# The first sorting in twelve held pieces, the reflections in a list of their own, and the fourth modulation over the dense stage

## The chip, the cores and the metric

The kernel runs on one core of one Trainium2 chip. A core has a matrix engine (PE, with its weight loads PEld), a vector engine (DVE), a scalar engine (ACT) and GpSimd (POOL). SP only issues DMAs, and POOL issues some too. Each engine works off its own queue in order, and semaphores tie the queues together. The metric is the device time of one execution in microseconds (us). The kernel before takes 1922.47 us, the median of three runs (1920.68 to 1925.31).

## The reference

Four blocks follow one another on `x`, 4 batches of 512 tokens of 288 features, with a condition row `c` for each batch:

```python
# block 0: attention, then a mixture of experts (4 experts, 2 for each token)
mod = silu(c) @ w_adaln + b_adaln              # six rows: shift, scale, gate, twice
x = x + g_msa * attention(ln(x) * (1 + sc_msa) + sh_msa)
xf = ln(x) * (1 + sc_mlp) + sh_mlp
cw = softmax over the top 2 of (xf @ w_gate), 0 for the other two
x = x + g_mlp * sum_e cw[e] * (gelu(xf @ w1[e] + b1[e]) @ w2[e] + b2[e])
# block 1: attention, then a dense MLP, modulated in the same way
# block 2: rotation in a subspace
U = qr(P).Q                                    # P is 288 x 64
R = expm(A - A.T), A's upper triangle = silu(c) @ W.T + b   # 64 x 64 for each batch
x = x + ((x @ U) @ R - x @ U) @ U.T
# block 3: as block 1, with LayerNorm weights ln1_w, ln1_b, ln2_w, ln2_b
```

Block 2's `qr` and `expm` don't depend on `x`: the kernel works them off in small pieces beside the blocks before. The six rows of `mod` of each block are as free.

## The kernel before

**Attention** (`attention`, run for blocks 0, 1 and 3 with names `a0`, `a1`, `a3`). There are 16 groups, 4 batches by 4 groups of 4 heads. A pass `r` computes the row maxima of group `r`, and the exponentials and sums of groups `r - 1` and `r - 2`. A pass has 8 gaps `k`. In each, `quad` puts two score tiles for maxima (`a0m`, reduced by DVE at L986) and two for weights (`a0s`, exponentials on ACT at L998) into four PSUM banks. Then come the pass's `steps[k]` and its `pieces`: letters that stand for generators advanced by one `yield` each (`Q` queries and keys, `X` values or projection, `A` transposed activations, `R` the sorting). Each pass ends with `shift`, four transposes (`a0sh`) that also mark passes in a trace. A tail of five steps follows pass 15: it finishes the last sums, starts the next feed's first chunks and the last projections.

**The feed** is what an attention hands over to: `Experts` after the first, `Dense` after the second and third. In `others` a feed streams matrix columns, and `went` calls `tick` each time that a number of columns, its pace, has passed.

**Side work.** `tick(works)` advances the first generator of a list by one `yield`. There are two lists: `beside`, begun with `rotation()`, and `aside`, begun with `exponential()`. In attention a tick of `beside` comes at some gaps (`ticks`: 4 a pass in the first attention, 2 from pass 10 on, 2 in the second), and in its tail. `rotation()` is 64 Householder reflections, then `subspace()` (the U of the reflections by a doubling of block sizes) and four products `ue`. A reflection's dots run on DVE, its root on POOL (`nrm`, L633; on DVE among the experts, where `far` is set); then DVE finishes it, and SP spreads a row over partitions (`v<-pT`, L550), which `reflect` applies on DVE. `modulation(l)` loads its matrix in six pieces, multiplies, and lays biases and LayerNorm rows out by many small DMAs on POOL's queue (`short_rows`, `features`: eight DMAs a table).

**Sorting.** `ranked(b)` computes a batch's gate logits and ranks, in 6 pieces; `placed(h)` counts how many tokens of a half of the batches each expert has, gives every token its slot, and issues the gathers (indirect DMAs on POOL) of the first experts' weights and tokens, in 6 pieces. The first half is sorted in passes 11 to 15 of the first attention, the second among the experts.

**Order.** A scheduler lays out each engine's queue from a model of times. What the kernel fixes: matmuls issued through `mm` stay in their order; `take(engine, i)` notes an instruction, and `beside_of(engine, j)` puts `j` behind the last one noted on that engine. The row maxima are noted for DVE. An instruction with neither can be placed ahead of a row maximum that comes before it in the program.

Of the kernel before, what the change touches and what calls it, by code (L numbers as in the profile page):

```python
# [8 lines left out]
F32 = mybir.dt.float32  # L9
# [37 lines left out]
def kernel(ctx: ExitStack, tc: tile.TileContext, a: dict, out: bass.AP):  # L47
# [53 lines left out]
    def beside_of(engine, instruction):  # L101
        if engine in taken:
            ordered(instruction.ins, taken[engine])

# [105 lines left out]
    def short_rows(dst, src, name, queue, got=None):  # L210

        n = src.shape[1]
        turned = small.tile([CP, KC, n], F32, tag=f"turned{n}", name=f"{name}t", bufs=1)
        early = got is not None
        if not early:
            got = small.tile([CP, n, KC], F32, tag=f"short{n}", name=f"{name}s", bufs=1)
            beside_of(queues.get(queue), queue.dma_start(got, src))
            beside_of("DVE", nc.vector.tensor_copy(turned, got.rearrange("p n k -> p k n")))
        else:
            in_turn("ACT", nc.scalar.copy(turned, got.rearrange("p n k -> p k n")))  # L220
# [102 lines left out]
    def modulation(l):  # L323
# [14 lines left out]
        def half(i):  # L338

            pieces, whole = [], l > 0 or i > 0  # L340
            if f"lnw{l}" in a:
                lnw = wt.tile([P, MC + 1, 2], F32, tag="lnw", name=f"lnw{l}_{i}")
                lnb = wt.tile([P, MC + 1, 2], F32, tag="lnb", name=f"lnb{l}_{i}")
                short_rows(lnw, a[f"lnw{l}"], f"lnw{l}_{i}", queue)
                short_rows(lnb, a[f"lnb{l}"], f"lnb{l}_{i}", queue)
            if whole and i == 0:
                nc.sync.dma_start(gate, a[f"adag{l}"].partition_broadcast(B))
            for n in range(3):
# [5 lines left out]
                if whole:  # L354
                    yield
            if i == 0:
# [214 lines left out]

    def reflect(k, m, v, n):
# [4 lines left out]
        nc.vector.scalar_tensor_tensor(w2[0:n], w, -1.0, c, ALU.mult, ALU.mult)  # L577
        nc.vector.scalar_tensor_tensor(
# [22 lines left out]
    def reflections():  # L601
# [14 lines left out]
        for k in range(RK):  # L616
# [27 lines left out]
            if n > 1:  # L644
                v = reflector("v", k)
                yield
                yield
                if far[0]:
                    yield
                    yield  # L650
                reflect(k, pT, v, n - 1)
# [229 lines left out]
    beside, aside = [rotation()], [exponential()]  # L881
# [7 lines left out]
    def attention(l, w, mod, eps, feed, ticks, hT=None, then=None, also=()):  # L889
# [11 lines left out]
        with ExitStack() as es:  # L901
# [353 lines left out]
            for r in range(1, n):  # L1255
# [4 lines left out]
                for k in range(gaps):  # L1260
# [17 lines left out]
                    if k % 2 and (k + 3) % (gaps // some) == 0:  # L1278
                        tick()

# [3 lines left out]
            for k in range(NT + 1):  # L1284
# [10 lines left out]
                if k < NT and k % (NT // ticks) == 0:  # L1295
                    tick()
            inside[0] = False
# [26 lines left out]
    class Feed:  # L1324
# [41 lines left out]

        def went(self, columns):
            for n, pace in enumerate(self.paces):
                self.streamed[n] += 0 if self.alone else columns
                if self.streamed[n] >= pace:  # L1370
                    self.streamed[n] -= pace
                    tick((beside, aside)[n])
# [134 lines left out]
    class Dense(Feed):  # L1507


        paces = (900,)  # L1510
# [47 lines left out]
    class Experts(Feed):  # L1558
# [90 lines left out]
        def modulated(self, b):  # L1649
# [20 lines left out]
            def scaled(t):  # L1670
# [7 lines left out]
                nc.vector.scalar_tensor_tensor(  # L1678
                    o, o, rstd[:, t : t + 1], rows["sh"], ALU.mult, ALU.add
                )  # L1680
                nc.vector.tensor_copy(
# [69 lines left out]
        def placed(self, h):  # L1751
# [7 lines left out]

            sel, upto = t3("sel", [HT, E]), t3("upto", [HT + 1, E])  # L1760
            nc.vector.tensor_scalar(sel, rank, 2.0, 1.0, ALU.is_lt, ALU.mult)
            nc.vector.memset(upto[:, 0, :], 0.0)
            for t in range(HT):
                nc.vector.tensor_add(upto[:, t + 1, :], upto[:, t, :], sel[:, t, :])
# [14 lines left out]
            def slots_of(o, v, n):  # L1779
# [3 lines left out]
                nc.vector.tensor_tensor(  # L1783
# [5 lines left out]
                nc.vector.tensor_reduce(o, over, AX.X, ALU.add)  # L1789

            def before(o, v):
                prior = t3("prior", [E, E])
                nc.vector.tensor_mul(prior, earlier, v.unsqueeze(1).to_broadcast(wide4))
                nc.vector.tensor_reduce(o, prior, AX.X, ALU.add)
# [5 lines left out]
            if h == 0:  # L1800

                taken, a_ = t3("taken", [E]), t3("a", [E])
                nc.vector.tensor_scalar_add(left, count, 1.0 - SW)
                slots_of(used, left, HB * T // SW)
                before(at, used)
                nc.vector.tensor_scalar(taken, at, -1.0, float(NF0), ALU.mult, ALU.add)
                nc.vector.scalar_tensor_tensor(taken, taken, 0.0, used, ALU.max, ALU.min)
                nc.vector.scalar_tensor_tensor(left, taken, -float(SW), count, ALU.mult, ALU.add)
                slots_of(g, left, HB * T // SW)
                before(starts[:, 0:E], g)  # L1810
                nc.vector.tensor_scalar(
                    a_, at, float(NF0), float(SW), ALU.min, ALU.mult
                )
                nc.vector.tensor_scalar_mul(b, taken, float(SW))
                nc.vector.tensor_scalar(
                    d, starts[:, 0:E], float(NF0), float(SW), ALU.add, ALU.mult
                )
                nc.vector.tensor_sub(d, d, b)
                nc.vector.tensor_sub(d, d, a_)
                firsts = at  # L1820
            else:
                nc.vector.tensor_add(used, left, count)
                slots_of(at, used, 2 * HB * T // SW)
                nc.vector.tensor_sub(used, at, g)
                before(at, used)
                nc.vector.scalar_tensor_tensor(d, at, float(SW), lk, ALU.mult, ALU.add)
                nc.vector.tensor_add(
                    starts[:, E : 2 * E], at, self.starts[:, 2 * E :].to_broadcast([P, E])
                )
                a_, b, firsts = la, lb, starts  # L1830
            pos, ge = t3("pos", [HT, E]), t3("ge", [HT, E])
# [4 lines left out]
            nc.vector.tensor_tensor(ge, ahead[:, 0:HT, :], each(b), ALU.is_ge)  # L1836
            nc.vector.tensor_mul(ge, ge, each(d))
            nc.vector.tensor_add(pos, ahead[:, 0:HT, :], each(a_))
            nc.vector.tensor_add(pos, pos, ge)
            yield  # L1840
            two, of = t3("pj", [2, HT]), t3("of", [HT, E])
            for j in range(2):
                for o, i in ((two[:, j, :], pos), (self.two[h][:, j, :], cw)):
                    nc.vector.scalar_tensor_tensor(
                        of, rank, float(j), i, ALU.is_equal, ALU.mult
                    )
                    nc.vector.tensor_reduce(o, of, AX.X, ALU.add)
            nc.vector.tensor_copy(self.place[h], two)
# [3 lines left out]
            nc.vector.tensor_tensor(  # L1852
# [5 lines left out]
            nc.vector.tensor_reduce(e, past, AX.X, ALU.add)  # L1858
            if h == 1:
                nc.vector.scalar_tensor_tensor(  # L1860
                    e, past[:, :, E - 1], -float(E), e, ALU.mult, ALU.add
                )
            nc.vector.tensor_copy(self.erow[h][:, 0:ns], e)
            nc.vector.scalar_tensor_tensor(
# [7 lines left out]
            if h == 0:  # L1872

                nc.vector.scalar_tensor_tensor(
                    la, starts[:, 0:E], float(SW), left, ALU.mult, ALU.add
                )
                nc.vector.scalar_tensor_tensor(lb, g, float(SW), left, ALU.mult, ALU.subtract)
                total = self.starts[:, 2 * E :]
                nc.vector.tensor_add(total, starts[:, E - 1 : E], g[:, E - 1 : E])
                nc.vector.tensor_add(lk, starts[:, 0:E], g)  # L1880
                nc.vector.tensor_sub(lk, total.to_broadcast([P, E]), lk)
                nc.vector.tensor_scalar_mul(lk, lk, float(SW))
# [9 lines left out]
            nc.vector.tensor_tensor(  # L1892
# [623 lines left out]
```

## Time and profile before

| | us |
|---|---|
| median of three runs | 1922.47 |
| the profiled execution, device time | 1925.5 |
| its span | 1923.8 |
| PE busy in the span | 1866.2 |
| first attention: first transposes of pass 0 to those of pass 15 (46.2 to 392.4) | 346.2 |
| second attention, the same (870.4 to 1190.2) | 319.8 |
| third attention, the same (1425.1 to 1740.8) | 315.7 |
| dense stage of block 1 after its first batch (1250 to 1385.7) | 135.7 |

A windows row reads: stretch from the span's start, its length, then busy time and number of instructions of each engine, the granted clock of PE, the DMA share and GB/s. "PE idle" and waits are what the trace shows between instructions of an engine, with what ended the wait. The three attentions have the same matrix work; the first and second also carry side work.

### The profile page before, as it was taken

What the parts mean: (1) busy time and instruction counts of PE and PEld (TensorE: products, weight loads), DVE (VectorE), ACT (ScalarE), POOL (GpSimd) and SP (SyncE); (2) the same over time, 40 slices, a digit from 0 to 9 for tenths busy, and PEclk for the clock granted to TensorE, in tenths of its full rate; (3) what the DMA queues carried; (4) which work ended last, traced back from release to release, by engine and by line L of the source; (5) the groups of instructions that cost most, each with busy time, mean ns of one, the idle gap of its engine ahead of it and who ended that gap; (6) DMA issues with size and microseconds to landing.
All of it is one profiled execution on the core that took longest, in us unless ns stands there. A gap on an engine that the chain in (4) does not pass through costs nothing. (4 is left out here: it accounts for less than half of the span.)

```text
span 1923.8 us, 28245 instructions
## 1 busy us (share of the span) xinstructions
PE 1866.2 (97%) x10385; PEld 993.9 (52%) x10385; DVE 1069.5 (56%) x3158; ACT 736.2 (38%) x1353; POOL 526.5 (27%) x766
## 2 busy tenths in 40 slices
PE   7999999989999999999999999999999999999998
PEld 4434444446767777774344443555654444433565
DVE  4677777735534555657867668152265666563201
ACT  1554554443322222324455555221134555455120
POOL 3021322234334347622313023112501121222101
PEclk9999999889989999999999999999999999999999
DMA  7421122325677667631211111300001111111000
GB/s 147 103 46 34 17 58 56 87 53 166 192 213 208 176 186 219 198 101 28 50 30 30 27 28 26 73 15 5 23 1 16 39 32 24 29 28 22 19 18 23
DMA packets 86988, 136.93 MB, mean 71 GB/s; under 512 B 32291, under 2 KB 67662, under 8 KB 86850
## 3 DMA queue, kind: packets, MB, share of 16 engines
q1 hardware_dynamic: 63554, 61.46, 14.3%
q0 software_dynamic: 23184, 73.66, 13.3%
q8 instruction: 82, 1.34, 0.3%
q14 instruction: 56, 0.46, 0.1%
q10 hardware_dynamic: 112, 0.01, 0.0%
HBM read 103.25 MB, written 20.08 MB: 64 GB/s over the span
## 5 line engine op out<-in xcount | busy, mean ns | idle before, releaser
L986 DVE TENSOR_REDUCE max<-a3m 128x1 f32<-128x512 f32 x256 | 164.7, 686 | 121.6 <-PE a3s L79 114.8
L986 DVE TENSOR_REDUCE max<-a1m 128x1 f32<-128x512 f32 x256 | 164.3, 684 | 88.2 <-PE a1s L79 82.1
L986 DVE TENSOR_REDUCE max<-a0m 128x1 f32<-128x512 f32 x256 | 165.2, 684 | 85.8 <-PE a0s L79 72.5
L998 ACT ACTIVATE a0p<-a0s 128x512 f32<-128x512 f32 x256 | 140.7, 596 | 155.2 <-PE a0s L79 155.0
L998 ACT ACTIVATE a1p<-a1s 128x512 f32<-128x512 f32 x256 | 140.0, 596 | 139.1 <-PE a1s L79 139.1
L998 ACT ACTIVATE a3p<-a3s 128x512 f32<-128x512 f32 x256 | 139.7, 596 | 135.5 <-PE a3s L79 135.5
L79 PE MATMUL e0h<-e0hT,e0w 128*128 128x256 f32 (+1 forms) x918 | 171.4, 400 | 2.3 <-ACT e0hT L2073 0.7
L79 PE MATMUL e0o<-e0w,e0hm 128*128 128x288 f32 x648 | 168.3, 409 | 2.4 <-DVE ef L854 2.4
L79 PE MATMUL a0m<-a0qk,a0qk 32*128 32x512 f32 x512 | 163.8, 649 | 6.6 <-DVE max L986 5.2
L79 PE MATMUL a0s<-a0qk,a0qk 32*128 32x512 f32 x512 | 166.5, 653 | 0.0
L79 PE MATMUL a1m<-a1qk,a1qk 32*128 32x512 f32 x512 | 153.3, 640 | 3.2 <-DVE max L986 1.8
L79 PE MATMUL a1s<-a1qk,a1qk 32*128 32x512 f32 x512 | 154.5, 639 | 0.0
L79 PE MATMUL a3m<-a3qk,a3qk 32*128 32x512 f32 x512 | 151.2, 640 | 2.3 <-ACT a3qk L969 0.8
L79 PE MATMUL a3s<-a3qk,a3qk 32*128 32x512 f32 x512 | 152.5, 640 | 0.0
L79 PEld LDWEIGHTS e0h<-e0hT,e0w 128*128 128x128 f32 (+1 forms) x918 | 130.5, 193 | 37.4 <-issue 16.7
L79 PEld LDWEIGHTS e0o<-e0w,e0hm 128*128 128x128 f32 x648 | 120.0, 190 | 33.9 <-DVE ef L854 3.1
L1424 ACT ACTIVATE e0hm<-e0h,e0w 128x256 f32<-128x256 f32 x144 | 60.1, 471 | 127.3 <-PE e0h L79 108.0
L633 POOL TENSOR_TENSOR nrm<-n,phalf 64x1 f32<-64x1 f32 (+34 forms) x35 | 19.3, 550 | 289.4 <-DVE n L628 289.4
L1984 POOL DMA_INDIRECT e0w<-w1c,wrow x57 | 55.6, 976 | 117.0 <-PE e0h L79 50.9
L79 PEld LDWEIGHTS a0m<-a0qk,a0qk 32*128 32x128 f32 x512 | 48.9, 185 | 68.8 <-DVE max L986 35.0
L79 PE MATMUL f1h<-f1hT,w 128*128 128x512 f32 (+1 forms) x216 | 81.3, 616 | 0.4 <-ACT f1hT L509 0.4
L79 PE MATMUL f3h<-f3hT,w 128*128 128x512 f32 (+1 forms) x216 | 79.4, 613 | 0.4 <-ACT f3hT L509 0.4
(532 smaller groups left out, 3184.9 us busy)
## 6 DMA issues: line engine op xcount, KB each, us to landing
eo<-e0r SPq DMA_DIRECT2D x50, 144.0 KB
ada<-in_ada SPq DMA_DIRECT2D x18, 324.0 KB
wr<-in_wrot SPq DMA_DIRECT2D x16, 288.0 KB
xm<-e0m SPq DMA_DIRECT2D x6, 768.0 KB
g<-gates SPq DMA_DIRECT2D x24, 144.0 KB
w<-in_w SPq DMA_DIRECT2D x6, 432.0 KB
x<-in_x SPq DMA_DIRECT2D x16, 144.0 KB
w1c<-in_w SPq DMA_DIRECT2D x8, 288.0 KB
```

What stands on the lines that cost most here:

```text
L79: ins = nc.tensor.matmul(*args, **kwargs).ins
L633: in_turn("POOL", nc.gpsimd.tensor_tensor(nrm, n2, phalf[0:n], ALU.pow))
L986: take("DVE", nc.vector.tensor_reduce(m[:, t, i, D : D + 1], ps, AX.X, ALU.max))
L998: take("ACT", nc.scalar.activation(p, ps, AF.Exp, scale=D**-0.5))
L1424: nc.scalar.activation(self.hms[i][f], ps[r], func, bias=b1(f)),
L1984: gather = nc.gpsimd.indirect_dma_start(dst, None, table, bass.IndirectOffsetOnAxis(row, 0))
```

## The change

**A list for the reflections.** `beside` begins empty and `rotation()` is in a new list, `turning`. In attention a tick of `turning` comes at gaps 1 to 6 of each pass for which `feed.turns(r)` holds and at which no `R` stands: passes 3 to 13 of the first attention and none in its tail, passes 5 to 15 of the second and two at each of the four steps of its tail. A reflection has one more `yield` before `reflect` (among the experts one of two extra ones goes in exchange, so five stay) and, inside an attention, one in the middle of `reflect` and one after it: six instead of three there, four instead of three in the dense stage. `went` ticks `turning` and `aside`; the dense stage's paces are 780 and 1900 columns, from one of 900.

**The fourth modulation** (`modulation(3)`) goes to `aside`, from `beside`, so that it runs beside the rotation over the dense stage. Its LayerNorm tables are loaded by POOL, copied on DVE some yields later, and spread one table a `yield`.

**The sorting.** `placed` has 12 pieces in place of 6, with these places for `R`:

```diff
-            if r == 13:
+            if r == 12:
                 loaded, steps = self.modulated(1)
                 loaded()
-                spaced([lambda k=k: (steps[k](), steps[k + 1]()) for k in range(0, 2 * NT, 2)])
+                spaced([lambda: None] * (NT - 1) + steps[0:NT])
+                self.scaled = steps[NT:]
+                pieces = {0: "XXX", 2: "XXQ", 3: "QQQ", 4: "QQQ", 6: "QQ"}
+            if r == 13:
+                spaced(self.scaled)
             more = {
                 11: {0: "R", 3: "R", 6: "R", 7: "R"},
-                12: {0: "R", 4: "R"},
-                13: {6: "R", 7: "R"},
-                14: {0: "R", 2: "R", 4: "R", 6: "R", 7: "R"},
-                15: {0: "R", 2: "R", 3: "R", 4: "R", 7: "R"},
+                12: {0: "R", 2: "R"},
+                13: {4: "R", 5: "R", 6: "R", 7: "R"},
+                14: {k: "R" for k in range(2 * NT)},
+                15: {k: "R" for k in range(6)},
             }.get(r, {})
```

**Held.** The DVE instructions of `choose`, `placed` and half of `modulated` go through `behind`, which puts each behind the last one noted on DVE. In the first sorting the running counts `upto` move from DVE to POOL, and a small copy of `modulated` (96 elements a partition) moves from DVE to ACT for the first two batches.

```diff
+    class Behind:
+        def __init__(self, engine, name):
+            self.engine, self.name = engine, name
+        def __getattr__(self, operation):
+            def one(*args, **kwargs):
+                ins = getattr(self.engine, operation)(*args, **kwargs)
+                beside_of(self.name, ins)
+                return ins
+            return one
+    behind = Behind(nc.vector, "DVE")
...
-    beside, aside = [rotation()], [exponential()]
+    turning, beside, aside = [rotation()], [], [exponential()]
...
+                    if 0 < k < gaps - 1 and feed.turns(r) and "R" not in pieces.get(k, ""):
+                        tick(turning)
...
+                for _ in range(2 if k < NT and feed.turns(n) else 0):
+                    tick(turning)
...
-                    tick((beside, aside)[n])
+                    tick((turning, aside)[n])
...
     class Dense(Feed):
-        paces = (900,)
+        paces = (780, 1900)
+        def turns(self, r):
+            return r > NG
...
+            other = nc.gpsimd if h == 0 else behind
-            nc.vector.tensor_scalar(sel, rank, 2.0, 1.0, ALU.is_lt, ALU.mult)
-            nc.vector.memset(upto[:, 0, :], 0.0)
+            behind.tensor_scalar(sel, rank, 2.0, 1.0, ALU.is_lt, ALU.mult)
+            other.memset(upto[:, 0, :], 0.0)
             for t in range(HT):
-                nc.vector.tensor_add(upto[:, t + 1, :], upto[:, t, :], sel[:, t, :])
+                other.tensor_add(upto[:, t + 1, :], upto[:, t, :], sel[:, t, :])
...
+        def turns(self, r):
+            return 2 < r < B * NG - 2
...
     mod, work = modulation(3)
-    beside.append(work)
+    aside.append(work)
...
     feed.finish()
+    while turning:
+        tick(turning)
     while beside:
         tick()
```

The old method `turns` of `Experts` is called `upright`. Among the experts the list of fine steps takes the twelve pieces of the second `placed` in the places of its six.

## The prediction

> **What bounds the kernel now.** First the busy shares and the clock of the page.
>
> ```profile
> PE 1866.2 (97%) x10385; PEld 993.9 (52%) x10385; DVE 1069.5 (56%) x3158; ACT 736.2 (38%) x1353; POOL 526.5 (27%) x766
> PEclk9999999889989999999999999999999999999999
> ```
>
> PE is busy for 97% of the span, so a gain must come from PE's idle time, from its slow stretches, or from matmuls that stretch while another engine is late. The clock dips in three places. The view of waits, PE alone, has the idle time:
>
> ```profile
> PE a0m L79 <- DVE max L986: 5.2, 9, 1.9
> PE e0xt L79 <- DVE a0r L1320: 4.6, 1, 4.6
> PE psr L786 <- DMA wr<-in_wrot: 3.4, 1, 3.4
> ```
>
> Then windows: the first attention's passes 1 to 14 and the third's, their last passes, and stretches of 3.41 us around the dips (stretch, length, busy us of PE, PEld, DVE, ACT, POOL; the clock stands third from the end).
>
> ```profile
> 46.20:359.40 313.20, 309.06 (x1919) 131.42 (x1917) 233.17 (x608) 157.44 (x280) 59.42 (x101) 1.00 0.23 52
> 1425.10:1721.00 295.90, 292.99 (x1817) 123.04 (x1815) 179.80 (x322) 153.14 (x272) 49.55 (x85) 1.00 0.14 27
> 359.40:392.40 33.00, 29.48 (x150) 13.38 (x149) 23.86 (x81) 10.37 (x19) 12.14 (x15) 0.79 0.44 116
> 1721.00:1740.80 19.80, 19.26 (x115) 6.51 (x113) 15.54 (x36) 9.78 (x18) 7.72 (x12) 1.00 0.13 18
> 369.17:372.58 3.41, 1.22 (x6) 0.40 (x6) 3.34 (x12) 0.45 (x1) 3.11 (x6) 1.00 0.93 287
> 372.58:386.24 13.66, 13.66 (x52) 6.56 (x56) 8.12 (x17) 2.92 (x6) 6.16 (x7) 0.50 0.56 165
> 406.72:410.13 3.41, 0.00 (x0) 0.00 (x0) 0.16 (x1) 1.30 (x4) 0.22 (x1) 1.00 0.42 40
> 410.13:420.37 10.24, 9.11 (x38) 2.46 (x38) 0.40 (x2) 1.46 (x3) 0.79 (x1) 0.50 0.14 15
> 734.39:737.80 3.41, 1.76 (x7) 1.44 (x8) 3.14 (x14) 0.00 (x0) 1.20 (x2) 1.00 0.79 218
> ```
>
> Pass 15 takes 33.0 us against 19.8 in the third attention. A stretch in which PE was busy for 1.22 of 3.41 us was followed by 13.66 us at half clock, one of 0.00 by 10.24 us; one of 1.76 was not. The timeline shows who was late, in pass 15 and in the tail (start, length, engine, line):
>
> ```profile
> 369.74 0.54 DVE L1892 TENSOR_TENSOR e0p0w<-e0p0pj,tiles 128x368 f32<-128x368 f32 x1
> 370.19 0.69 DVE L986 TENSOR_REDUCE max<-a0m 128x1 f32<-128x512 f32 x1
> 370.93 0.69 PE L79 MATMUL a0m<-a0qk,a0qk 32*128 32x512 f32 x1 [1.93 <-DVE max L986]
> ...
> 405.95 0.55 SPq L550 DMA_DIRECT2D v<-pT  x1
> 406.61 0.61 SPq L1070 DMA_DIRECT2D a0den<-a0raw  x1
> ...
> 409.97 0.25 DVE L1081 RECIPROCAL a0den<-a0den 128x16 f32<-128x16 f32 x1 [4.04 <-DMA a0den<-a0raw]
> 410.14 0.40 DVE L1320 TENSOR_TENSOR a0r<-a0pp,g 128x288 f32<-128x288 f32 x1
> 410.59 0.69 PE L79 MATMUL e0xt<-ident,e0x 128*128 128x128 f32 x2 [4.61 <-DVE a0r L1320]
> ```
>
> In pass 15 sorting instructions ran in a row ahead of a row maximum, and PE's scores waited for its bank. In the tail a0raw was written by 399.4, but its DMA `a0den` went out at 406.6, behind a reflection's `v` on SP's queue, which waited for POOL and DVE; the reciprocal waited for a0den, the projection's `a0r` stood behind it on DVE, and PE waited for that bank.
>
> **Sorting, pass 15.** Of the 13.2 us over the third attention's pass, the sorting's own matmuls take 0.63 (e0p0n) and 3.92 (e0p0k, twice 1.96 at full clock). The other 8.65 us are the stall and the half clock. After the change DVE's sorting work there is pieces 7 to 12, about 7 us (wide ones 0.54, 0.51, 0.52, 0.58 and twice 1.22; some fifteen small ones of 0.17); with 16 maxima of 0.684, the 0.69 of L1040 and 1.2 of projection and reciprocal that is 19.8 of 24.3 us, no piece over 1.7. I take **-8.65**; bounds -10.5 (the rest of DVE's lag too) and 0 (the burst is as long when held).
>
> The Trainium skill ("TensorE: Matmul & The Clock Gate", section "Why this matters for your kernels") asks only that no idle gap pass about 3 us. By it the gap of 1.93 us would have kept the clock and its removal would bring some 2 us, not 8.65; the rows above show the clock halved after it, and the measurement decides.
>
> **Sorting, pass 14.** Six pieces of `placed` come in. DVE: maxima 10.9, L1040 0.69, divides 2.2, reciprocal 0.25, `choose` 2.3, `sel` and 31 small ones of 0.17 5.6: 21.9 us, against 20.1 of the third attention's pass 14 plus 0.7 of matmuls: **+1.1** (0 to +2.5). `upto` on POOL is not in the trace as such. Its nine instructions lie between a memset of 128x4 at 0.10 (L114) and a power of 128x4 at 1.03 (L471); nearest in work is a copy of 64x64 at 0.25 (L753), so 2.1 us. POOL first has four DMA issues (2.05) after a0raw, which was there at 345.4, so `upto` ends at 349.6; the counting matmul stands at the end of gap 3, at 348.4 (338.0 and four gaps of 2.6) to 350. **+0.5**; ends 0 and +6.5 (power's price: 355.8). Behind that matmul stand all of PE's scores, the copy `ahead` on DVE and so the maxima. Batch 1's modulation a pass earlier moves two row loads and one store on SP and the projection's matmuls in pass 12; as many instructions, nothing late behind them (its `x` is complete after gap 2): 0. ACT's eight copies (a 128x128 one took 0.27) lie under ACT's idle half: 157 of 313 us busy; uncovered 2.2. The first weight gathers (seven of 0.97 on POOL) go out in gap 3 of pass 15, some 5 us later against the passes than now (366.3), and are first needed by e0h in the tail, at 413: 17 us of cover.
>
> **Tail.** No `v` on SP: a0den goes at 399.5, its reciprocal runs by 403, a0r follows, and nothing holds e0xt at 406. Gone are 4.61 us and half of the 9.11 us of work at half clock, 4.56: **-9.2**. Late next would be the second a0den, which feeds a projection 17 us further on. Bounds -9.7 and 0 (another wait there keeps the clock low).
>
> **First attention, passes 1 to 14.** 313.2 against 295.9 is 17.3 us; modulation 1.64, ranks 1.62 + 0.99 + 1.68 + 0.99 and `psback` 0.70 are matmuls of its own, 7.7 with small ones. The other 9.6 go with DVE's 53 us of extra work. Ticks: counting yields, 47 ticks of three a reflection, 15.7 reflections, become 60 ticks of six: 10. A reflection is 3.06 us of DVE (0.44, 0.43, 0.48 and a dozen of 0.07 to 0.21), so 17.4 us go, a third: -3.1; and the largest burst falls from 2.15 us to 0.9, within the 1.2 us that the maxima leave in a gap of 2.6. **-4.0** (-8 to 0).
>
> **Moved reflections.** Second attention: eleven reflections and part of a twelfth as before, now in passes 5 to 15 and smaller pieces; it is 4.2 us over the third: **-1.0** (-3 to +1.5). Experts: 146 ticks of five as now, 0. Dense stage: 58752 columns (three batches of 9x2x512 + 4x9x288) in 135.7 us, 433 a us; 75 ticks of 1.80 us for 12.5 reflections (four each), 22 of `subspace`, 4 of `ue`: done at tick 73, not drained. The chain from `sn` (1266.34) to the applied row's start (1269.34) takes 3.0 us of the 5.4 of three ticks. The modulation's 18 ticks of 4.4 us end well before. A wait of 0.70 us for `mod` goes: **-0.7** (-2 to +4).
>
> **Sum.** -8.65 + 1.1 + 0.5 - 9.2 - 4.0 - 1.0 - 0.7 = -21.95, from 1925.5 of the profiled execution: 1903.5. The median of the runs is 3.0 below that execution: **1900.5 us**, with its own range 1893 to 1909.
>
> **Rivals.** *The load of `wr` comes in time too.* PE waited 3.45 us for it at 553 and then worked 10.13 us at half clock: 8.5 us, so 1892. Against it: its DMA went out at 541.6 with the DMA engines full (share 1.03 at 530 to 540), and that traffic and its pace stay.
>
> *A stall of the old size at a new place.* `upto` at the power's price, +6, and a dip, +5; or a `v` ahead of a1den in the second tail, where eight ticks stand for two, at the old price 4.6 + 4.6. For: 1200.58 shows a `v` just ahead of a1den. Against: PE lost nothing there. About 1910.
>
> *Slower: POOL's bursts in the dense stage.* The modulation's five tables are eight DMA issues of 0.51 each, 4.1 us of POOL. They ran after the rotation; now `nrm` queues behind them, `sn` heads DVE's queue waiting, and behind it the sums that free PE's three banks. A tile of f1o takes 2.18 us (17.47 for eight), so two free banks cover 4.4. Without that cover each burst costs 4.1 and a dip of 5.1: 46 us, 1946. It decides from two and a half such bursts (22 us).
>
> *The hold does not do what it says*: pass 15 stays at 33 us; 1909, in the upper end of the range.
>
> **Chances.** Forecast 0.54, `wr` 0.12, new stall 0.18, slower 0.12, no hold 0.04. The range, 1887 to 1920, leaves out the slow case and little else. A change under 0.2% (1918.6 to 1926.3) can't be told from none here: faster 0.82, same 0.05, slower 0.13.
>
> **What would show it.** Pass 15 at about 24 us and no half clock between the first sorting's passes and the expert start; e0xt without a wait for a0r; passes 6 to 10 nearer 21.4; ten reflections before the experts; `wr`'s wait still there. A new half-clock stretch in pass 14, in the second tail or in the dense stage would make it wrong, as would a rotation unfinished when the dense stage ends.

## The result, and the profile after

The changed kernel takes 1929.56 us, the median of nine runs (1922.96 to 1936.4); the kernel before, run beside it, 1921.51 (1915.13 to 1927.51). The ratio is 1.0043, with a 95% interval of 1.0023 to 1.0063: slower by some 8 us, where 22 us less were forecast. The profiled execution of the changed kernel took 1936.4 us, the longest of its nine, span 1934.7, against 1923.8 for the span of before: 10.9 us more, to be found below. In the experiments each ratio is to the kernel before, run beside that group; between groups, compare the ratios and not the medians.

First the busy shares and the clock of the changed kernel's page.

```profile
PE 1871.3 (97%) x10385; PEld 1001.3 (52%) x10385; DVE 1071.4 (55%) x3152; ACT 737.5 (38%) x1361; POOL 530.4 (27%) x774
PEclk9999999998889999999999999999999999999999
```

PE has as many matmuls as before and is busy 5 us longer; it stands at half clock for 61.4 us of the span, where it was 34.1. The dip that stood in slices 8 and 9 (end of the first attention, and its tail) is gone, and the one in slice 12 has become a wider one in slices 10 to 12, which are the experts. The view of waits, PE alone (what it waited for, us in all, times, the longest):

```profile
PE psr L827 <- DMA wr<-in_wrot: 6.2, 2, 3.4
...
PE pss L855 <- DVE ef L888: 4.2, 1, 4.2
...
PE a0m L79 <- DVE max L1027: 3.8, 7, 1.0
PE e0p1k L79 <- DVE e0p1h L112: 2.5, 1, 2.5
...
PE e0p0n L79 <- POOL e0p0upto L1817: 1.1, 1, 1.1
...
PE a1s L79 <- DVE sn L678: 0.9, 1, 0.9
```

The two waits that the change was to remove are gone: `e0xt` is not in the list, and the longest wait of `a0m` fell from 1.9 us to 1.0. Longer or new are `psr` (3.4 before), `pss` (at most 1.2 before), `e0p1k`, the second sorting's matmul, and two small ones. Windows of the changed kernel, one row a stage: first attention, its tail up to the first matmul `e0r2t` of batch 2's ranks, from there to the last `psr`, the rest of the experts, second attention, and from there to the third.

```profile
47.42:386.13 338.71, 330.75 (x2067) 141.62 (x2066) 248.33 (x609) 167.98 (x305) 73.26 (x121) 0.99 0.26 59
386.13:443.75 57.62, 55.86 (x276) 32.99 (x275) 14.36 (x44) 21.85 (x46) 26.04 (x33) 0.97 0.30 78
443.75:581.84 138.09, 127.01 (x681) 95.32 (x682) 61.34 (x330) 36.90 (x80) 47.14 (x48) 0.86 0.65 184
581.84:879.55 297.71, 289.60 (x1693) 221.40 (x1691) 159.02 (x704) 73.48 (x173) 134.93 (x146) 0.99 0.60 176
879.55:1197.08 317.53, 312.56 (x1930) 130.02 (x1928) 230.43 (x544) 162.87 (x289) 77.91 (x121) 1.00 0.16 33
1197.08:1436.06 238.98, 233.69 (x1012) 131.24 (x1011) 106.70 (x413) 58.45 (x97) 68.32 (x120) 0.99 0.10 24
```

The third row has the loss: its clock is 0.86, and the stretch took 121.1 us before. The clock is halved there for 37.5 us: 10.2 from 445.3 on, after small waits of `e0r2t`; 13.65 from 503.4, after `e0p1k`; 13.65 from 558.0, after `psr`. Before, it was 10.2 us, after `psr` alone. The same six lengths for the kernels that the experiments need, read from the same matmuls in each trace (us, one profiled execution each):

| kernel | first attention | tail to `e0r2t` | to the last `psr` | rest of the experts | second attention | to the third |
|---|---|---|---|---|---|---|
| before | 346.2 | 64.4 | 121.1 | 292.4 | 319.8 | 234.9 |
| changed | 338.7 | 57.6 | 138.1 | 297.7 | 317.5 | 239.0 |
| changed, again | 338.2 | 57.4 | 137.8 | 296.4 | 317.6 | 239.5 |
| changed, second sorting free | 336.5 | 57.5 | 123.1 | 295.0 | 317.5 | 238.9 |
| sorting part alone | 340.2 | 60.6 | 135.8 | 290.5 | 319.8 | 235.4 |
| sorting part alone, second free | 343.1 | 62.2 | 120.8 | 292.5 | 321.4 | 235.2 |
| before, wqk later | 343.3 | 61.7 | 113.7 | 296.4 | 319.7 | 235.3 |
| best: sorting, second free, wqk later | 343.7 | 60.5 | 112.5 | 293.8 | 319.8 | 235.2 |

By this table the 10.9 us of the two profiled executions are: first attention -7.5, tail -6.8, then +17.0, +5.3, -2.3 and +4.1, and +1.2 ahead of the first attention.

What PE waits for in the third row is in the timeline of the changed kernel (start, length, engine, line, operation):

```profile
495.67 0.40 ACT L2172 COPY e0r<-e0o 128x288 f32<-128x288 f32 x1 [1.79 <-PE e0o L79]
496.10 0.46 DVE L2173 TENSOR_TENSOR e0r<-e0r,e0b 128x288 f32<-128x288 f32 x1 [2.87 <-ACT e0r L2172]
496.48 0.18 DVE L112 SCALAR_TENSOR_TENSOR e0p1of<-rank,e0p1pos 128x32 f32<-128x32 f32 x1
...
498.19 0.63 DVE L112 TENSOR_TENSOR e0p1w<-e0p1pj,tiles 128x464 f32<-128x464 f32 x1
...
500.65 1.22 DVE L112 TENSOR_TENSOR e0p1h<-e0p1lane,lanes 128x1024 f32<-128x1024 f32 x1
502.02 2.37 PE L79 MATMUL e0p1k<-e0p1w,e0p1h 128*128 128x28 f32 x16 [2.50 <-DVE e0p1h L112]
```

L112 is the line in `Behind` through which every held instruction goes. `contract`'s addition of an expert's bias, `e0r` at L2173, is noted on DVE, and it waits for ACT's copy of a product that PE has only just finished: DVE stood idle for 2.87 us. The second sorting is held behind that addition; its last pieces then run one after another from 496.48 to 501.87, and PE waits for the end of them. The 2.37 us that `e0p1k` takes is itself partly at half clock, which lasted 13.65 us from 503.4.

And for `pss`:

```profile
637.08 0.62 SPq L584 DMA_DIRECT2D v<-pT  x1
...
643.03 0.14 DVE L588 COPY v<-v 41x1 f32<-41x1 f32 x1 [5.33 <-DMA v<-pT]
643.10 0.21 DVE L886 COPY ef<-m 128x128 f32<-128x128 f32 x1
...
647.12 0.61 DVE L888 COPY ef<-psm 64x128 f32<-64x128 f32 x2
647.46 1.44 PE L855 MATMUL pss<-ef 64*64 64x64 f32 x16 [4.18 <-DVE ef L888]
```

DVE stood for 5.33 us on a reflection's `v`, then worked off that reflection with its root, and only then the copies of `ef` that PE was waiting for.

### The profile page after: what moved, and what is told of

The parts are those of the page before. It is cut to its first block, busy times and chain, and to the rows that moved or that the text cites. A ratio compares the mean times of both kernels' runs of the same rounds, so it can differ in the third digit from the quotient of the medians.

```text
span 1934.7 us, 28257 instructions
## 1 busy us (share of the span) xinstructions
PE 1871.3 (97%) x10385; PEld 1001.3 (52%) x10385; DVE 1071.4 (55%) x3152; ACT 737.5 (38%) x1361; POOL 530.4 (27%) x774
## 4 chain that ended last, share of the span: by engine, by line
PE 72%; DVE 8%; DMA 3%; issue 1%; POOL 1%; ACT 1%; SPq 0%; POOLq 0%; DVEq 0%; ACTq 0%
PE av L79 8%; PE a3m L79 7%; PE a1m L79 7%; PE e0o L79 7%; PE e0h L79 6%; PE a3psqk L79 4%; PE a1psqk L79 4%; PE f1h L79 4%; PE f3h L79 4%; PE f1o L79 4%; PE f3o L79 4%; DVE max L1027 3%; PE a0m L79 2%; DMA v<-pT 1%; PE a3psv L79 1%
## 5 line engine op out<-in xcount | busy, mean ns | idle before, releaser
L79 PE MATMUL e0h<-e0hT,e0w 128*128 128x256 f32 (+1 forms) x918 | 176.1, 413 | 1.0 <-ACT e0hT L2141 0.5
L79 PE MATMUL a0m<-a0qk,a0qk 32*128 32x512 f32 x512 | 156.6, 642 | 5.4 <-DVE max L1027 3.8
L79 PE MATMUL a0s<-a0qk,a0qk 32*128 32x512 f32 x512 | 158.0, 642 | 0.0
L1472 ACT ACTIVATE e0hm<-e0h,e0w 128x256 f32<-128x256 f32 x144 | 60.5, 471 | 134.0 <-PE e0h L79 120.6
L2052 POOL DMA_INDIRECT e0w<-w1c,wrow x57 | 55.8, 979 | 127.0 <-PE e0h L79 64.4
L673 POOL TENSOR_TENSOR nrm<-n,phalf 64x1 f32<-64x1 f32 (+33 forms) x34 | 18.8, 553 | 237.9 <-DVE n L668 237.8
L79 PEld LDWEIGHTS a0m<-a0qk,a0qk 32*128 32x128 f32 x512 | 47.1, 183 | 62.2 <-DVE max L1027 35.4
```

Of the source, the lines that this page charges most:

```text
L79: ins = nc.tensor.matmul(*args, **kwargs).ins
L673: in_turn("POOL", nc.gpsimd.tensor_tensor(nrm, n2, phalf[0:n], ALU.pow))
L1472: nc.scalar.activation(self.hms[i][f], ps[r], func, bias=b1(f)),
L2052: gather = nc.gpsimd.indirect_dma_start(dst, None, table, bass.IndirectOffsetOnAxis(row, 0))
```

## The experiments

**Is it the hold on the second sorting?** The change goes through `behind` everywhere; this run takes it from the half that is sorted among the experts, and from the ranks and the modulation of that half's two batches.

```diff
         def placed(self, h):
...
+            held = behind if h == 0 else nc.vector
...
-            behind.tensor_scalar(sel, rank, 2.0, 1.0, ALU.is_lt, ALU.mult)
+            held.tensor_scalar(sel, rank, 2.0, 1.0, ALU.is_lt, ALU.mult)
...
```

> The changed kernel, with the second sorting and the modulation and ranks of batches 2 and 3 (the ones that run among the experts) no longer held behind DVE's last taken instruction; the first sorting stays held. Theory A (the time was lost among the experts because the hold reaches the second sorting: the matmul e0p1k waited 2.50 us behind the expert's add, then 13.65 us at half clock; e0r2t waited 2.1 us, then 10.2 us at half clock): both go, 9.3 and up to 7 us, so the median falls from 1929.6 to 1913 to 1920, and no wait of e0p1k over 1 us is left. Theory B (it was lost because the reflections stand at another place among the experts: `v` on SP between the loads of wr, and DVE standing on `v` ahead of ef): no change, 1926 to 1933, and psr's 6.2 us and pss's 4.2 us remain.

1917.51 us, 0.9992 of before (0.9974 to 1.0011). The stretch to the last `psr` fell from 138.1 to 123.1 us, and `e0p1k` does not wait; `psr` still waits 6.2 us. The stretch as a window, then the order that did it, from the timeline:

```profile
439.39:562.49 123.10, 113.44 (x681) 85.35 (x682) 61.08 (x329) 36.69 (x80) 46.16 (x48) 0.97 0.71 206
```

```profile
487.25 0.63 DVE L1952 TENSOR_TENSOR e0p1w<-e0p1pj,tiles 128x464 f32<-128x464 f32 x1
...
488.46 0.62 DVE L1962 TENSOR_TENSOR e0p1w<-e0p1w 128x448 f32<-128x448 f32 x1
488.99 0.45 DVE L2174 TENSOR_TENSOR e0r<-e0r,e0b 128x288 f32<-128x288 f32 x1
...
490.05 1.22 DVE L1971 TENSOR_TENSOR e0p1h<-e0p1lane,lanes 128x1024 f32<-128x1024 f32 x1
```

Free, the sorting fills the time in which DVE stood idle, and `e0r` comes in the middle of it. The same on the other half of the change: the sorting part alone on the reflections of before, held and free.

> The kernel before with the sorting part alone: twelve held pieces, batch 1's modulation a pass earlier, upto on POOL, the grouped pieces among the experts; the reflections, their yields, their paces and the fourth modulation as before. The stall in pass 15 (8.65 us forecast, 7.8 measured in the changed kernel) should go; the tail's a0den stays late. Theory A: the experts lose 9 to 16 us as in the changed kernel, so 1922 to 1930. Theory B: the experts keep the time of before, so 1912 to 1916 against 1921.5.

> The kernel before with the sorting part alone, the first sorting held, the second sorting and the modulation and ranks of batches 2 and 3 not held; the reflections as before. It is to the run of the sorting part alone (1.0021 of before) what the run with the second sorting free is to the changed kernel, on the other half of the change. Theory A (the hold on the second sorting is the cost): 10 to 14 us less than with it held, 0.994 to 0.997 of before; e0p1k waits under 1 us, and the stretch from the last psr of the experts back to e0p1k is some 71 us, not 79. If that gain was chance or belongs to the new places of the reflections: 1.000 to 1.004 as with the hold.

Held 1924.71 us, 1.0021 (0.9999 to 1.0042), with `e0p1k` waiting 3.47 us; free 1919.83 us, 0.9993 (0.9977 to 1.0009). The stretch falls from 135.8 to 120.8 us. So the hold on the second sorting costs 15 us in that stretch in each of the two pairs of profiled executions, and by the ratios 10 and 5 us of the whole; in the second pair the two intervals overlap. The other executions on the new reflections agree: 137.8 us held, and 122.8 to 125.6 in five more with the second sorting free (128.1 in a sixth, the half tick below). In the changed kernel some 9.3 of the 15 us are `e0p1k` itself, 2.5 of wait and half of the 13.65 at half clock; the rest is half clock elsewhere in the stretch, whose length and place differ between executions. Theory A holds for that much. With no hold anywhere:

```diff
-    behind = Behind(nc.vector, "DVE")
+    behind = nc.vector
```

> The changed kernel with no instruction of either sorting held: the twelve pieces, their places and everything else as changed. If the hold is what ended pass 15's stall, pass 15 is 33 us again and the half clock of some 13 us behind it is back (8 us); if the smaller pieces did it alone, pass 15 stays at 25 us. Theory A: the experts gain 9 to 16 us besides, so 1921 to 1929 with the stall and 1913 to 1920 without. Theory B: 1937 with the stall, 1929 without.

1923.66 us, 1.0009 (0.999 to 1.0028). Passes 14 and 15 took 26.3 and 25.2 us, against 22.0 and 25.2 in the changed kernel: the smaller pieces in their new places ended the stall of pass 15 without the hold, and the hold is worth some 4 us in pass 14, in this one execution. The stretch to the last `psr` is 124.8 us, as theory A has it; the time is above its 1913 to 1920.

**The other half.** The reflections' list, yields and paces, with the old sorting:

> The kernel before with the reflections' part alone: their own list, none in the first attention's tail, the added yields, paces 780 and 1900, the fourth modulation over the dense stage; the sorting as before. The tail's wait and half clock (9.2 us) should go; pass 15 keeps its stall. Theory A: the experts keep the time of before, so 1908 to 1914 against 1921.5. Theory B: the experts lose some 15 us by wr, ef and the half clocks behind them, so 1922 to 1930.

1920.93 us, 0.9996 (0.9982 to 1.001). The tail took 59.6 us and the stretch after it 124.2, 3 more than before; the second attention 323.2 with a new wait of 1.68 us in its last pass, and 237.5 follow. What the tail gave is paid back in three places, and neither theory's range held.

**Three mends on the new reflections.** From the kernel with the second sorting free: the nine loads of the next attention's weights later, no ticks in the second tail, and both with one more piece in the first sorting.

```diff
-                at(NS // 2 + n, 4, load)
+                at(NS // 2 + 2 + n, 4, load)
...
-            return r > NG
+            return NG < r < B * NG
```

> The kernel of the run with the second sorting free (1917.5), with the next attention's nine weight loads two expert items later, so that wqk's megabyte no longer goes out some 10 us ahead of the loads of wr that psr waits for. If those loads stand in the way: the waits of psr (0.97 and 5.18 us) and the 6.8 us of half clock behind them go, 1908 to 1911. If the expert's own gathers are what fills the DMA engines: psr waits as before and the time stays at 1915 to 1920. The load of `bv` and `bp`, which stood ahead of a `v` on SP's queue before pss's wait (2.42 us), also moves; if it was the cause, that wait shrinks by 1.5 to 2.4 us.

> The kernel of the run with the second sorting free (1917.5), with no tick for the reflections in the second attention's tail and 720 columns a tick in the dense stage for 780. If the eight ticks in that tail cost the 0.98 + 0.88 us of waits and the 6.8 us of half clock there: about 5 us less, 1911 to 1914, and the stretch from the last a1sh to the first a3sh falls from 238.9 to 234 us. If the dense stage's faster pace makes a wait of its own: 1917 to 1922.

> Both edits of the two runs beside it, and one more piece in the first sorting (a gap between upto on POOL and the matmul that counts, so that e0p0n's wait of 1.12 us and the 3.4 us of half clock behind it go, 2.8 us). If each is additive: 1917.5 - 8 - 5 - 2.8 = 1902; if half-clock stretches only move to other places: 1911 to 1917.

All three missed: 1921.83 us, 1.0004 (0.9983 to 1.0026); 1924.07 us, 1.0021 (1.0 to 1.0042); 1928.06 us, 1.0034 (1.0012 to 1.0056). With the loads later `psr` still waited, 4.8 us, and the last loads now went out among the next modulation's, for which PE waited 5.11 us. Without ticks in the second tail `a1sh` and `a1s` waited as before, 0.98 and 1.12 us. With the extra piece pass 14 fell to 20.1 us and pass 15 rose to 29.3: `a0m` waited 1.53 us there.

> The kernel before with the nine weight loads two expert items later. If wqk stands in wr's way there too: psr's 3.45 us and most of the 10.2 us of half clock go, 1912 against 1920. If the gathers do: 1920. Its first 480 us are instruction for instruction those of the kernel before, so it also shows how far pass 15's stall and the tail's keep their half clock from one execution to the next: about 13.7 and 10.2 us if these are the kernel's own, other lengths if they are chance.

1921.03 us, 0.9999 (0.9978 to 1.0019). Here the stretch lost its wait for `wr` (115.6 us), and PE waited 2.54 us for the modulation's load instead. The run says more about the forecast. The first attention and the tail run the instructions of before, and took 343.6 + 61.7 = 405.3 us, where the execution on which the forecast was made had 346.2 + 64.4 = 410.6. The stall of 1.93 us in pass 15 is there again, at the same place; the half clock after it is 6.8 us at first, not 13.7, but 10.2 and 3.4 us follow further on, in all 20.5 us in these two stretches for 23.9; and `e0xt` waited 0.78 us, not 4.61.

**On the reflections of before.** With the sorting part and the second sorting free: only wqk's load later; no ticks of reflections in the first tail; both.

```diff
-                at(NS // 2 + n, 4, load)
+                at(NS // 2 + n + (0 if n else 2), 4, load)
```

> The same, with only wqk's load two expert items later. With all nine loads later, the kernel before lost psr's wait for wr (3.9 us of waits to 1.4, 10.2 us of half clock to 3.4) and paid again where its last loads met the modulation's (psada waited 2.54 us). With wqk alone moved nothing is put onto the modulation: if that is right, 6 to 8 us less than the run beside it, 0.990 to 0.993 of before. If relief there only turns up as another wait: the same as the run beside it.

> The run beside it with the second sorting free, without the four ticks of the first attention's tail; that shifts every later reflection by a tick or more. The tail (from the last a0sh to e0r2t) took 64.5 us in the profile of before, 61.7 in another execution of the same instructions, 57.6 in the changed kernel. If the reflection there is what holds a0den: 57 to 58 and 3 to 6 us less than the run beside it. If the new places among the experts matter (theory B: `v` between the loads of wr, `v` ahead of ef), the waits of psr or pss grow by 3 us or more and the time does not fall.

> Both edits of the two runs beside it. If they add: 9 to 14 us less than the run with the second sorting free on the old reflections, 0.985 to 0.990 of before. If half-clock stretches follow any small wait wherever it moves: within 3 us of the best of the two alone.

Wqk alone: 1912.54 us, 0.9956 (0.9936 to 0.9976), `psr` without a wait. No ticks in the tail: 1919.82 us, 0.9983 (0.997 to 0.9996); the tail went from 62.2 to 59.0 us, not to 57, and the later reflections moved by a tick, after which PE waited 1.22 us for `skew` and 2.00 for the modulation. Both: 1915.6 us, 0.9972 (0.9953 to 0.9991), no better than wqk alone: `psr` waits again, 2.54 us, and `pst` 3.07 us.

**What the reflections' new places cost.**

> The changed kernel with the second sorting free and wqk's load alone two expert items later. On the old reflections the same edit took 7.3 us off (1919.8 to 1912.5) and psr's wait was gone. If wqk is what held wr here too: psr's 6.2 us and the half clock behind it go, 0.994 to 0.996 of before. If the reflections' `v` among the loads of wr holds them (theory B): psr keeps 3 us or more of waits, 0.998 to 1.000.

> The run beside it, with the second attention's ticks for reflections in passes 4 to 14 in place of 5 to the tail, and 740 columns a tick in the dense stage for 780. With the ticks out of the tail alone a1sh and a1s still waited 0.98 and 1.12 us, with 6.8 us of half clock. If a reflection begun in the last pass is what is late there: both waits go and the stretch from the last a1sh to the first a3sh falls from 239 to 235 us, 4 us less than the run beside it. If something else is late there: the waits stay and the time is the same or longer.

> The run of the second sorting free with wqk later, with the experts' count for the reflections begun at 600 columns, half a tick early. Before, seven of DVE's instructions stand between ef's first copy and the two that pss waits for; as changed, seventeen, the chain of a reflection and its `v` among them; here seven again. If that order makes pss wait (2.4 to 4.2 us in the profiles as changed, under 0.85 to 1.2 before): the wait is under 1.3 us and the half clock behind it goes, 3 to 6 us less than the first run of the four. If not, pss waits on.

> The changed kernel itself once more, no edit, on the same chip as the three beside it. The verdict should repeat, 1.002 to 1.006 of before. What belongs to the kernel (the waits of e0p1k, 2.5 us, psr, 6.2 us, pss, 4.2 us, a1sh and a1s) should be there again within half a us; the half clock behind each (3.4 to 13.7 us) may differ, and that difference is chance.

Wqk later on the new reflections: 1927.91 us, 1.0029 (1.0008 to 1.0049), and `psr` waits 4.13 us. That is slower than either theory had it: the edit that was worth 7 us on the old reflections is worth nothing on the new ones. In this trace `v` goes out on SP at 530.5 and the three loads of `wr` at 531.3, 534.9 and 538.0, 3.5 us before PE wants them; in the version without a wait (wqk alone, old reflections) the loads go out at 532.2, 534.4 and 535.7, 11 us before. Ticks taken out of the second attention's pass 15 and tail and put into its pass 4: 1928.05 us, 1.0027 (1.001 to 1.0045); `a1s` no longer waits and `a1sh` waits 0.54 us, as before the change, but the stretch to the third attention is 241.1 us all the same: a matmul of the modulation in the dense stage now waits 2.01 us for DVE.

Half a tick earlier: 1944.33 us, 1.0105 (1.0072 to 1.0138), where 3 to 6 us less were expected. The wait of `pss` is gone, as expected, and the second attention takes 336.2 us, for 319.2 in the first run of the four. Its waits and its timeline show why:

```profile
PE a1sh L79 <- DVE max L1027: 12.8, 12, 3.5
```

```profile
1026.02 3.04 POOL L1149 TENSOR_TENSOR x<-x,a1bg 128x288 f32<-128x288 f32 x4
...
1026.80 0.77 DVE L678 SCALAR_TENSOR_TENSOR sn<-sgn,nrm 22x1 f32<-22x1 f32 x1
...
1027.61 0.71 DVE L679 TENSOR_TENSOR pT<-pT,sn 22x1 f32<-22x1 f32 x1
...
1028.36 0.72 DVE L680 TENSOR_TENSOR den<-sn,pT 22x1 f32<-22x1 f32 x1
...
1029.11 0.14 DVE L681 TENSOR_SCALAR den<-den 22x1 f32<-22x1 f32 x1
...
1029.79 1.27 DVE L1027 TENSOR_REDUCE max<-a1m 128x1 f32<-128x512 f32 x2
...
1031.11 0.48 PE L79 MATMUL a1sh<-ident,max 128*128 128x128 f32 x1 [2.03 <-DVE max L1027]
```

Inside an attention a reflection now has six yields, and a pass of the second attention has six ticks. So every pass works off one reflection, and each step of it falls at the same gap in pass after pass, wherever the experts happened to leave it. In the changed kernel `sn` falls 6 us into a pass; here it falls 19 to 27 us into it, among the last maxima, on which `shift` waits.

The changed kernel once more took 1934.29 us, 1.0067 (1.0045 to 1.0088), just over the expected range. Its waits:

```profile
PE psr L827 <- DMA wr<-in_wrot: 5.8, 2, 3.1
...
PE e0p1k L79 <- DVE e0p1h L112: 2.5, 1, 2.5
PE pss L855 <- DVE ef L888: 2.5, 1, 2.5
```

All of them are there again, `pss` shorter by 1.7 us. The stages repeat within 1.5 us, and the half clock behind `psr` and `e0p1k` too (13.65 us each).

**A version that beats both.** Wqk's load later on the kernel before, with nothing of the change, and the best version once more:

> The kernel before with wqk's load alone two expert items later, and nothing of the change. psr's wait for wr (3.45 us) and its 10.2 us of half clock should go. If the sorting in held pieces is worth the 7 us that were forecast for it: 0.995 to 0.997 here and 0.992 to 0.994 in the run beside it. If it is worth little on the old reflections (0.9993 when measured with the second sorting free): the two are within 2 us of each other.

> The best version so far once more: the sorting of the change with only the first sorting held, the old reflections, wqk's load alone later. The 0.9956 of before should repeat, 0.994 to 0.997, with psr not waiting.

1915.95 us, 0.9973 (0.9959 to 0.9987), and 1913.16 us, 0.9954 (0.9936 to 0.9971). The load accounts for some 6 us between medians. The sorting with the second half free gives 3 more, but the two intervals overlap. The window of the best version from `e0r2t` to the last `psr`:

```profile
449.76:562.24 112.48, 110.21 (x681) 84.13 (x682) 59.86 (x313) 36.86 (x80) 47.49 (x49) 1.00 0.74 216
```

The same 681 matmuls as in the third row above, at full clock throughout: 112.48 us for 138.09.

## Why the prediction was wrong

**The step that failed** is the one that gave the experts no price: "Experts: 146 ticks of five as now, 0". The prediction followed the hold through the first sorting alone. But `behind` is in `choose`, `placed` and `modulated`, which serve both halves, and among the experts the last instruction noted on DVE is an addition that waits for PE and ACT. Held behind it, the second sorting became the kind of burst that the hold was to break up: `e0p1k` waits 2.5 us, the clock halves, and with the later `psr` the stretch is 17 us longer; the rest of the experts is another 5.3 longer. So a term of 0 measured 22.3 us, two thirds of the 32.9 us that lie between the forecast's -21.95 and the +10.9 of the profiled executions. Taking the hold away gives 15 of these back in two pairs of traces. But the changed kernel without it is only as fast as the kernel before (0.9992), so the hold is not the whole miss; the rest is in the places and sizes below. None of the rivals on record had the hold reach the experts; the one that ended slower, POOL's bursts in the dense stage, was not seen.

**The count of ticks was right and beside the point.** Ten reflections were done before the first tail, as counted; in the kernel before it was fourteen, where the prediction counted 15.7. But with that, other reflections meet other work there: `pss` waits behind one (4.2 and 2.5 us), and wqk's load no longer decides about `psr`. That the places alone can make a difference is shown by the half tick, in the second attention: 16 us between the medians of two kernels run side by side (1927.91 and 1944.33) that differ in one starting count. For the experts, the half tick took `pss`'s wait away, as the order of DVE's instructions had it. Which order of `v` and `wr` makes `psr` wait is argued from two traces and not shown.

**Two sizes were one execution's.** The forecast's -8.65 for pass 15 and -9.2 for the tail named the right waits: pass 15 took 25.2, 26.3 and 23.5 us in three executions of the new first attention (24.3 forecast), though the pieces did it and not the hold, and `e0xt` waits no more. As sizes they came from one execution. In two others of the old instructions (all nine loads later, and wqk's alone, on the kernel before) pass 15 took 30.1 us, not 33.0, `e0xt` waited 0.8 us, not 4.61, and first attention and tail together took 405 us, not 410.6. From those 405 us the changed kernel's 396.3 and 395.6 are 9 us away, where the sum had 20.25 for these parts.

**Smaller terms.** Pass 14: the eight additions of `upto` took 2.40 us on POOL and ended at 351.3, and the matmul waited 1.1 us, for the 0.5 forecast; good. Passes 1 to 14: 313.6, 311.9 and 313.0 us against 313.2, so the -4.0 was hardly there, with DVE 3.2 us less busy there: four reflections fewer, not 5.7, and more of the sorting. That PE was not waiting for this work is argued. Second attention: -2.3 for -1.0. Dense stage: +4.1 for -0.7, and the timeline of the changed kernel shows it in the second tail:

```profile
1198.48 1.89 DVE L521 TENSOR_SCALAR ln_0xn<-x,ln_0mv,ln_0rstd 128x256 f32<-128x256 f32 x2
...
1200.29 0.67 DVE L1081 TENSOR_TENSOR a1qk<-a1qk,a1sh 128x512 f32<-128x512 f32 x1
1200.89 0.16 DVE L678 SCALAR_TENSOR_TENSOR sn<-sgn,nrm 14x1 f32<-14x1 f32 x1
```

The list of waits puts the 0.9 us of `a1s` down to `sn`, but `a1qk`, which is part of the scores' input, runs just ahead of it; with no ticks in that tail `a1s` waited 1.12 us for `a1qk`, with no `sn` there. What is late is `a1qk`: the two `ln_0xn` ahead of it took 1.89 us while POOL worked on `nrm`, `a1bg` and `x`, and 0.66 us at this place in the kernel before, where POOL was idle. A reflection's dots in pass 15 also stand ahead of the last maxima there, for which `a1sh` waits 0.98 us, and 6.8 us at half clock begin at 1199.7. With pass 15's ticks moved to pass 4 the two `ln_0xn` took 0.66 us again and `a1s` did not wait, but a wait in the dense stage cost as much. The prediction's count of ticks in the dense stage was off too: by its own figures 50 + 22 + 4 are 76, one more than the 75 ticks there, and not 73. The last `ue` began at 1391.2, still ahead of the stage's last matmul at 1395.3.

**Two rivals in part.** A new wait in the second tail was named, at 4.6 + 4.6 us; it came, at 4.1 in all, by DVE and not by `v` ahead of a1den. The load of `wr` was priced at 8.5 us if it came in time; on the kernel before, wqk's load later brings it in time and the median falls by 5.8 us. The change itself does not touch that load.

**What stays open.** Between the kernels on the new reflections with the second sorting free, medians ran from 0.9992 to 1.0034 of before, the half tick aside, with edits that should not have cost anything. And the sum of the two halves measured alone, +0.21% and -0.04%, is less than the +0.43% and +0.67% of both; the pairs of stalls that meet were not taken apart further.

## What to carry to other kernels

A helper that orders instructions behind "the last one noted" must be followed to every place that calls it: what it holds them behind there may itself be waiting. A count of ticks is not enough to say that moved side work costs nothing: look at which instruction each step now stands ahead of, above all where a round has as many ticks as a piece of work has yields (six and six here), which locks each step to one place. And a stall's half clock should be priced from more than one execution.

## What was not expected of the hardware

The granted clock halves for stretches of 3.41, 6.83, 10.24 or 13.65 us, once 17.07 (sorting part alone), multiples of one length, and how many follow the same wait changes between executions: 13.65 us in one and 6.83 in two others directly after the 1.93 us of pass 15. The Trainium skill ("TensorE: Matmul & The Clock Gate", section "What's actually happening") describes a window of 3413 ns in which the busy share is judged, which runs freely and does not start with the kernel. The lengths agree with that; that the window's position makes the executions differ is not shown here. Its rule of thumb in the section "Why this matters for your kernels", no idle gap over about 3 us, does not cover what is seen here: `e0p1k`'s 2.50 us was followed by 13.65 us at half clock in both executions.

In the timeline of the half tick, DVE's operations on 22 elements with two inputs took 0.77, 0.71 and 0.72 us while POOL added 128x288 tiles. In the same trace the instructions of these three lines that no operation of POOL overlapped, 170 of them, took 0.12 to 0.18 us. The Trainium skill ("GPSIMD Engine Reference", section "Specifications") names contention of POOL with DVE instructions that have two inputs in SBUF; the rows agree with it, at some 0.6 us for each such instruction.
